# One product with B's row for two groups, in a selective-scan kernel on Trainium2

## The chip, the cores and the metric

The kernel runs on one core of a Trainium2 chip. The metric is the device time of one execution in microseconds; of the kernel before there are three runs, whose median is given below. A profile of a further execution shows each instruction of the engines: PE (TensorE, matmuls), DVE (VectorE), ACT (ScalarE), POOL (GpSimd) and SP, which here issues DMAs.

## What is computed

Four layers act on an image of 4 x 56 x 56 tokens with 96 channels. The first two hold a selective scan in four directions over the image; the last two are attention (linear, without a softmax) and a small quantised feed-forward net, per token. Nearly all of the time goes to the two layers with scans. Cut to what matters, each scan is, per image, direction, channel d (192 of them) and state s (16):

```python
d_a = jnp.exp(dt[..., None] * a)              # decay, per token, channel and state
d_b = dt[..., None] * b_ssm[:, :, None, :]    # B's row, the same for all channels

def step(h, inp):
    da_t, db_t, x_t, c_t = inp
    h = da_t * h + db_t * x_t[..., None]
    y_t = jnp.einsum('bds,bs->bd', h, c_t)
    return (h, y_t)
_, ys = jax.lax.scan(step, h0, xs)
```

The scan runs over 3136 tokens. The input of state s at a token is dt * x (one value for each channel) times B (one value for each state).

## The kernel before

**Tiling.** The 3136 tokens are cut into seven chunks of 448. A round takes one chunk, one half of the channels (e, 96 of 192) and a quarter of the states (q, four of 16): 96 x 4 = 384 pairs of channel and state, as three groups g of 128 partitions. With 2 layers x 4 images x 4 directions x 7 chunks x 2 halves x 4 quarters there are 1792 rounds. The order of the instructions on PE, ACT, DVE and POOL is written out by hand in `scans`; the other work of the layers (norms, projections, convolutions, attention) runs beside as "lanes", which step between the pieces of a round by a planner's budget.

**A round n**, engine by engine:

- PE spreads B's row over the 128 partitions: a matmul with a selection matrix leaves it in the PSUM tile `b` (L606, `spread_b`, one buffer). It is issued in `begin(n + 1)`, in the middle of the round before.
- POOL makes the input of group 2 in `begin` (L699): `du` (dt * x, from a DMA) times B's row from SBUF.
- DVE makes the inputs of groups 0 and 1 in `products` (L704): two instructions, each 128 x 448, `du` from SBUF times `b` from PSUM, written into the tile `h`. In `h` each group has its own row of 450 columns (`ROW`, 448 tokens and two more), so that the carry of the chunk before can lie beside the tokens. `tokens(h)` is the view of its 448 tokens by group.
- DVE then runs three scans in place (L711), one for each group: they read the decay `da[g]` (PSUM, one buffer per group) and the input in `h`, and overwrite `h` with the states. The state begins from the carry column beside the tokens.
- ACT computes the decay of the next round's group g after the scan of group g has freed `da[g]` (L663, `decay`), saves the last column of h (L681, `kept`) and puts the carry into the tile of round n + 2 (L676, `carried`). `h` has three buffers.
- POOL multiplies the states by C's row (L753, `hc`), and PE sums them over the states into `y` (L784, `add_up`), two rounds later. PE also runs matmuls on zeros (L771) in a number that the planner sets.

On DVE the order in a round is: product of group 0, product of group 1, scan 0, then what the lanes have for DVE, scan 1, scan 2. The products and the first scan always follow one another directly.

Of the kernel before, what the change touches and what calls it, by code (L numbers as in the profile page):

```python
# [16 lines left out]
ALU = mybir.AluOpType  # L17
# [15 lines left out]
CS = 448  # L33
# [134 lines left out]
class Net:  # L168
# [444 lines left out]
    def scans(self):  # L613
# [7 lines left out]
        nc, sp = self.nc, self.sp  # L621
        chunks = []
        for l in range(2):
            for i in range(NB):
                for n, (orient, rev) in enumerate(ORDER[l]):
                    for step in range(NCS):
                        ch = Step()
# [55 lines left out]
        def own(n):  # L683
            ch, e, q = rounds[n]
            return NQ * e + q in (OWN_TAIL if ch.l and ch.i else OWN)

        hs, bs = {}, {}

        def tokens(t):

            return self.groups(t, 2)[:, :, :CS]
# [8 lines left out]

        def products(n):
            ch, e, q = rounds[n]
            for g in range(3 if own(n) else 2):
                nc.vector.tensor_tensor(tokens(hs[n])[:, g], ch.du[e][:, g], bs[n], ALU.mult)  # L704

        def scan(n, g):
            ch, e, q = rounds[n]
# [13 lines left out]
        for n, (ch, e, q) in enumerate(rounds):  # L721
            r = NQ * e + q
            products(n)
            for c, o in steps(n):
                self.prepare(c, o)
# [669 lines left out]
```

## Time and profile before

| | us |
|---|---|
| median of 3 runs (8209.97 to 8214.31) | 8210.29 |
| the profiled execution, its own time | 8208.04 |
| its span, first to last instruction | 8206.3 |
| granted TensorE clock, mean over the span | 0.895 |
| L753 on POOL, 1792 products with C's row | 4883.6 |
| L663 on ACT, 5376 decays | 3353.4 |
| L784 on PE, 14336 sums over the states | 1924.6 |

The profile's first part gives, for each engine, the time in which it was busy, its share of the span, and the number of its instructions. A row of the groups reads: line, engine, operation, what is written and read, shape, count, then busy time in all and mean nanoseconds of one instruction, then the idle time of the engine just before such instructions and what ended it. An instruction's own length can overlap that of the next on the same engine, so the mean times the count can be more than the busy time. In the timeline each row gives the start and the length in microseconds from the span's start; rows of the same kind that follow one another are merged, with their count, and an idle gap before them is shown with what ended it. The rounds run from about 120 to 7926 us of the span; before lies the setup, after it the last lanes.

### The profile page before, as it was taken

Reading aid. Unit: us, or ns where it says so; the run is one execution under the profiler, and the core shown is the slowest. Engines: PE = TensorE matmul, PEld = TensorE weight load, DVE = VectorE, ACT = ScalarE, POOL = GpSimd, SP = SyncE. Lnnn points to the kernel's source line nnn. Section 1 sums busy time; section 2 is a strip of 40 time slices with the busy share of each in tenths; the row PEclk is TensorE's granted clock in tenths of the full one; section 3 lists DMA queues with packets and bytes.
Section 4 is the critical chain, followed back from the end, with each engine's and each line's share of the span. In section 5 each row is a group of like instructions: output and inputs, shape, how many; then the busy total and the mean of one; then the engine's idle time right before and its main releaser. Section 6 shows DMA issues by size and latency. Waiting matters only on the chain.

```text
span 8206.3 us, 113425 instructions
## 1 busy us (share of the span) xinstructions
PE 7235.6 (88%) x33734; PEld 2586.3 (32%) x33734; DVE 7506.3 (91%) x9558; ACT 6104.9 (74%) x12807; POOL 7170.8 (87%) x3991
## 2 busy tenths in 40 slices
PE   7889988889888988889898989998898988989897
PEld 3333333222332223322332224332343323433345
DVE  5999999999999999999999998999989999899961
ACT  5778877787778767886777866787767786677755
POOL 4999999999999998999999997999989998899950
PEclk8899989899999988999899998989889898898976
DMA  4566655567556665566565665555655555555531
GB/s 148 176 195 192 199 186 181 176 195 230 178 183 190 204 195 182 180 198 197 194 192 181 210 204 172 168 169 176 196 164 169 165 176 185 167 172 164 179 115 49
DMA packets 568241, 1467.55 MB, mean 179 GB/s; under 512 B 108034, under 2 KB 337156, under 8 KB 566756
## 3 DMA queue, kind: packets, MB, share of 16 engines
q1 hardware_dynamic: 566848, 1458.49, 56.2%
q8 instruction: 265, 4.34, 0.2%
q14 instruction: 356, 2.92, 0.1%
q10 hardware_dynamic: 772, 1.80, 0.1%
HBM read 1186.49 MB, written 273.47 MB: 178 GB/s over the span
## 4 chain that ended last, share of the span: by engine, by line
PE 34%; DVE 30%; ACT 16%; issue 13%; POOL 4%; DMA 2%; SPq 0%; DVEq 0%; POOLq 0%; ACTq 0%
DVE h L711 22%; PE y L784 7%; DVE h L704 7%; PE y L771 5%; ACT da L663 5%; PE y L780 4%; PE b L606 3%; POOL hc L753 2%; PE pp L486 2%; ACT L815 2%; PE pp L440 2%; PE ps L923 1%; PE ps L836 1%; PE ps L851 1%; ACT Y L791 1%
## 5 line engine op out<-in xcount | busy, mean ns | idle before, releaser
L711 DVE TENSOR_TENSOR_SCAN h<-da,h 128x449 f32<-128x449 f32 (+1 forms) x5376 | 5506.4, 1071 | 97.8 <-ACT da L663 83.5
L753 POOL TENSOR_TENSOR hc<-h,cb 128x1344 f32<-128x1344 f32 x1792 | 4883.6, 2725 | 616.2 <-DVE h L711 474.3
L663 ACT ACTIVATE da<-dt,na 128x448 f32<-128x448 f32 x5376 | 3353.4, 632 | 1116.2 <-DVE h L711 1086.0
L704 DVE TENSOR_TENSOR h<-du,b 128x448 f32<-128x448 f32 x3584 | 2016.1, 603 | 135.9 <-PE b L606 72.9
L784 PE MATMUL y<-hc,four 128*32 128x448 f32 x14336 | 1924.6, 612 | 17.5 <-POOL hc L753 17.5
L699 POOL TENSOR_TENSOR h<-du,cb 128x448 f32<-128x448 f32 x1792 | 1753.2, 978 | 70.4 <-ACT h L676 27.6
L771 PE MATMUL y<-w,zeros 128*96 128x448 bf16 x5112 | 1426.5, 398 | 0.0
L606 PE MATMUL b<-cf,sel 128*128 128x448 bf16 x1792 | 677.6, 378 | 691.4 <-DVE h L704 685.2
L771 PEld LDWEIGHTS <-zeros 128*96 128x96 bf16 x5112 | 633.6, 135 | 1178.0 <-issue 1018.7
L440 PE MATMUL pp<-U,wd 96*128 96x448 f32 x896 | 669.2, 835 | 11.7 <-issue 4.6
L784 PEld LDWEIGHTS y<-hc,four 128*32 128x32 f32 x14336 | 295.0, 113 | 1201.0 <-issue 684.6
L780 PE MATMUL y<-Y,ident 96*96 96x448 f32 x672 | 541.4, 895 | 36.3 <-ACT Y L791 19.2
L486 PE MATMUL pp<-cf,wd 12*96 12x448 f32 (+1 forms) x896 | 477.7, 615 | 87.7 <-ACT dtc L496 53.7
L681 ACT COPY carry<-h 128x3 f32<-128x3 f32 x1536 | 302.0, 197 | 261.5 <-DVE h L711 255.7
L511 POOL TENSOR_TENSOR duc<-dtc,U 96x896 f32<-96x896 f32 x224 | 482.9, 2156 | 4.4 <-ACT dtc L498 4.4
L791 ACT COPY Y<-y 96x448 f32<-96x448 f32 x448 | 342.1, 764 | 27.6 <-PE y L784 26.4
L676 ACT COPY h<-carry 128x3 f32<-128x3 f32 x1536 | 279.9, 182 | 51.5 <-POOL hc L753 48.4
L496 ACT ACTIVATE dtc<-pp,wd 96x448 f32<-96x448 f32 x448 | 281.5, 628 | 21.5 <-PE pp L486 17.4
L836 PEld LDWEIGHTS ps<-avg,w 96*112 96x112 f32 (+1 forms) x2008 | 264.6, 197 | 98.1 <-issue 55.4
L606 PEld LDWEIGHTS <-sel 128*128 128x128 bf16 x1792 | 184.7, 103 | 351.4 <-issue 282.4
L577 ACT COPY cf<-pp 64x448 f32<-64x448 f32 x448 | 235.6, 526 | 70.1 <-PE pp L599 61.5
L851 PEld LDWEIGHTS ps<-ident,rs 112*96 112x96 f32 x1808 | 224.0, 186 | 134.8 <-issue 92.2
(376 smaller groups left out, 5712.9 us busy)
## 6 DMA issues: line engine op xcount, KB each, us to landing
cb<-cd SPq DMA_DIRECT2D x896, 448.0 KB, 4.6
dt<-dd SPq DMA_DIRECT2D x448, 672.0 KB, 5.7
du<-dd SPq DMA_DIRECT2D x448, 672.0 KB, 5.7
dd<-dtc SPq DMA_DIRECT2D x672, 112.0 KB, 2.0
dd<-duc SPq DMA_DIRECT2D x672, 112.0 KB, 2.0
win<-m SPq DMA_DIRECT2D x252, 112.0 KB, 4.0
U<-u SPq DMA_DIRECT2D x112, 168.0 KB, 4.7
w<-z SPq DMA_DIRECT2D x84, 224.0 KB, 4.4
```

The source lines that it names most:

```text
L440: self.nc.tensor.matmul(ch.ps.rearrange("p (a b) -> p a b", b=HS), ch.par.wx[:, e], self.in_order(self.U[e], ch.orient, ch.c * CS, CS), st ...
L486: self.nc.tensor.matmul(ch.pd, ch.par.wt[rows, C * e : C * e + C], ch.cf[rows], start=True, stop=True)
L511: self.nc.gpsimd.tensor_tensor(in_rows(ch.duc), in_rows(ch.dtc), u[:, :, lo : lo + CS // HS], ALU.mult)
L606: self.nc.tensor.matmul(ps, self.sel[:, q], self.upper(ch.cf), start=True, stop=True)
L663: nc.scalar.activation(da[g][:, INNER], ch.dt[e][:, g], AF.Exp, scale=ch.par.na[:, e, q, g : g + 1])
L699: nc.gpsimd.tensor_tensor(tokens(hs[n])[:, 2], ch.du[e][:, 2], ch.cb[q][:, 1], ALU.mult)
L704: nc.vector.tensor_tensor(tokens(hs[n])[:, g], ch.du[e][:, g], bs[n], ALU.mult)
L711: nc.vector.tensor_tensor_scan(h[:, way], da[g][:, way], h[:, way], 0.0, ALU.mult, ALU.add)
L753: nc.gpsimd.tensor_tensor(hc, tokens(hs[n]), ch.cb[q][:, 0].unsqueeze(1).to_broadcast([128, NG, CS]), ALU.mult,)
L771: self.nc.tensor.matmul(self.y[:C], self.zeros[:, :C], self.some, start=False, stop=False)
L780: nc.tensor.matmul(o, w, self.in_order(a, ch.orient, ch.c * CS, CS), start=True, stop=False)
L784: nc.tensor.matmul(self.y[32 * n : 32 * n + 32], self.four, hc[:, g], start=n == 3, stop=n == 3 or q == NQ - 1,)
```

## The change

The two instructions of `products` become one. It writes both groups of h (two rows of 448, 450 apart), reads both groups of `du`, and reads B's row in PSUM twice: the view has a middle dimension of length m with a step of zero. (`own` is false in every round of this kernel, so m is 2.)

```diff
         def products(n):
             ch, e, q = rounds[n]
-            for g in range(3 if own(n) else 2):
-                nc.vector.tensor_tensor(tokens(hs[n])[:, g], ch.du[e][:, g], bs[n], ALU.mult)
+            m = 3 if own(n) else 2
+            b = bs[n].unsqueeze(1).to_broadcast([128, m, CS])
+            nc.vector.tensor_tensor(tokens(hs[n])[:, :m], ch.du[e][:, :m], b, ALU.mult)
```

Nothing else is changed. The built program has 1792 fewer instructions on DVE. The first scan still waits for DVE's own semaphore and for ACT's; the second, which waited for both, now waits for ACT's alone; the third waits for ACT's and POOL's, as before. The merged product carries the waits that the two had: PE's (B's row), ACT's (the carry) and, where a chunk begins, a DMA's (`du`).

## Prediction

> **What bounds the kernel now.** I read the page first: the sums by engine, then its costliest groups.
>
> ```profile
> span 8206.3 us, 113425 instructions
> PE 7235.6 (88%) x33734; PEld 2586.3 (32%) x33734; DVE 7506.3 (91%) x9558; ACT 6104.9 (74%) x12807; POOL 7170.8 (87%) x3991
> ...
> L711 DVE TENSOR_TENSOR_SCAN h<-da,h 128x449 f32<-128x449 f32 (+1 forms) x5376 | 5506.4, 1071 | 97.8 <-ACT da L663 83.5
> ...
> L704 DVE TENSOR_TENSOR h<-du,b 128x448 f32<-128x448 f32 x3584 | 2016.1, 603 | 135.9 <-PE b L606 72.9
> ```
>
> DVE is the fullest engine, and L704 and L711 are nearly all of it: two products and three scans in each of 1792 rounds. The stretches view puts the rounds between 120 and 7926 us of the span, with DVE busy for 7444.6 of those 7806 us: 4.356 us a round, and only 361 us idle in all. The three-engine balance (PE 88%, POOL 87%) doesn't change this: where DVE hardly idles, time added to it lengthens the run, up to those 361 us.
>
> Next I read the timeline of DVE alone, in the middle (start, length, both in us):
>
> ```profile
> 4020.40 1.12 DVE L704 TENSOR_TENSOR h<-du,b 128x448 f32<-128x448 f32 x2
> 4021.44 3.05 DVE L711 TENSOR_TENSOR_SCAN h<-da,h 128x449 f32<-128x449 f32 x3
> 4024.41 1.12 DVE L704 TENSOR_TENSOR h<-du,b 128x448 f32<-128x448 f32 x2
> ```
>
> A round without a stall takes 4.01 us (4020.40 to 4024.41), less than 2 x 0.603 + 3 x 1.071 = 4.42. So an instruction begins before the one ahead has ended: the pair ends at 4021.52, its first scan begins at 4021.44, 0.08 us sooner. Taken one by one, the second product starts 513 ns after the first and the scan 531 ns after that: 1044 ns from the first product to the scan. This is the number that the change replaces. 1150 of the 1792 rounds are within 0.1 us of this pace.
>
> **The part that goes.** One instruction and its fixed cost. What one longer instruction takes comes from these three lengths, all with one operand in PSUM:
>
> ```profile
> L227 DVE TENSOR_TENSOR in<-in,ps 96x384 f32<-96x384 f32 x2 | 1.1, 550 | 1.3 <-PE ps L226 1.3
> ...
> L405 DVE TENSOR_TENSOR qkv<-w,ps 96x288 f32<-96x288 f32 x2 | 0.9, 452 | 1.7 <-PE ps L404 1.7
> ```
>
> Slope (550 - 452) / 96 = 1.02 ns an element, so 448 more cost 457 ns. A first product without a stall takes 593 ns and the mean is 603, so the merged one takes 1050 to 1060; I take 1055. No product with two rows of 448 and a zero step over PSUM is in the trace. The bounds are 1050 and, if a new row paid the whole start again, 593 + 593 = 1186 ns. I take the low end's side because the one small product of this shape (L326, 96x8 as two rows of four, the second operand repeated by a zero step) takes 0.16 us, as does a product of one element: rows and the zero step cost nothing there.
>
> **The part that is added: a wait.** The first scan reads and overwrites group 0 of h. Before, group 0 was written by the first product, which ends half a microsecond ahead of the scan's start; the second product covered the wait. Merged, group 0 is not complete until the whole instruction is, and the built program has the scan wait for DVE's semaphore directly behind it. No DVE instruction of another kind stands between products and scan in any round, and the changed program has none there either, so nothing covers it. What a waiting instruction costs is shown in the setup:
>
> ```profile
> 3.60 0.16 DVE L342 TENSOR_TENSOR bn1t<-c 96x1 f32<-96x1 f32 x1 [0.85 <-DMA c<-in_c_dram]
> 3.68 0.15 DVE L342 TENSOR_TENSOR bn2t<-c 96x1 f32<-96x1 f32 x1
> ...
> 5.79 0.15 DVE L341 TENSOR_TENSOR bn1s<-bn1s,c 96x1 f32<-96x1 f32 x1
> 5.98 0.15 DVE L343 TENSOR_TENSOR bn1t<-bn1t,bn1s 96x1 f32<-96x1 f32 x1
> 6.17 0.15 DVE L344 TENSOR_TENSOR bn1t<-bn1t,c 96x1 f32<-96x1 f32 x1
> ```
>
> The two L342 are independent: the second starts 0.08 before the first ends. L341, L343 and L344 feed each other: each starts 35 ns after the end ahead (0.04 as rounded). But they wait for one semaphore. The scan waits for two (the product, and ACT's decay factors), and the sequencer takes the first as a step of its own (an event of 21 ns, 5286 of them on L711). In the trace this event, for the first product, comes 38 ns after that product's end. What follows a late event is seen where a product waits for B's row from PE:
>
> ```profile
> 983.91 0.36 PE L606 MATMUL b<-cf,sel 128*128 128x448 bf16 x1
> ...
> 984.31 0.62 DVE L704 TENSOR_TENSOR h<-du,b 128x448 f32<-128x448 f32 x1 [0.39 <-PE b L606]
> ```
>
> ```profile
> 295.11 0.57 PE L606 MATMUL b<-cf,sel 128*128 128x448 bf16 x1
> ...
> 295.79 0.62 DVE L704 TENSOR_TENSOR h<-du,b 128x448 f32<-128x448 f32 x1 [1.19 <-PE b L606]
> ```
>
> At 984 PE ends at 984.27 and the product starts 0.04 later, by a direct wait. At 295 an event lies between (PE ends at 295.68): 0.11 later. In all 19 waits of that kind the product starts 44 or 45 ns after the event. So the scan starts 38 + 21 + 44 = 103 ns behind the product's end; the bounds are 35 (the wait for the product is the direct one) and 108 (the event case as seen from PE). I take 103, since the program lists the two waits in the same order as before, where the product's was the event. Below nothing is a case of its own, under the rivals.
>
> A scan that starts on an idle engine also pushes the next a little: 1009 ns to the second scan in the 157 rounds where the first had stalled, against 1002: 7 ns.
>
> **Other moves.** The second scan loses its wait for DVE, which was long met: nothing. B's row on PE is freed when the products end; measured from the products' start that is 1.12 us before and 1.055 after, and the next row is due some 3 us later: nothing. The merged product takes over the second one's wait for ACT's carry, set 3 us ahead (copied at 4021.18, used at 4024.41): nothing, or 70 ns in some of the 87 waits for PE, 6 us at most. PE, ACT and POOL have the same instructions in the same order. On SP some DMA issues move a few places; DVE's waits for du come to 26.8 us, 19.2 of them at the first, so I put this at nothing, within 10 us either way.
>
> **The sum.** A round in step: 1055 + 103 + 7 - 1044 = 121 ns more. If all 1792 paid: 217 us. A round that stalls anyway, for ACT, PE or a DMA, takes the delay out of its stall. 386 rounds have an idle gap over 20 ns. If each covers itself, 1406 pay (170 us); if each covers the round ahead too, 1020 pay (123 us). I take 1200: 145 us. Against the profiled execution's own 8208.0 us (span 8206.3) that is 8353, and the median of the runs shown lies 2 us above that execution: 8355.
>
> **A rule against this sum.** The Trainium skill, VectorE: DVE Perf Modes, sections "The DRAIN you can't avoid" and "Rules for kernel authors", says that a semaphore after each chained Vector instruction costs nothing extra and that one should lower the count of instructions, not of semaphores. By it the scan would follow the merged product as it follows the second one now, 80 ns before its end: 975 - 1044 = -69 ns a round, 124 us faster. The setup's rows speak otherwise: 0.08 us before the end without a wait and 0.04 after it with one.
>
> **Rivals.**
> - The direct wait: 35 ns in place of 103. 53 ns a round; 1200 x 53 = 64 us: 8274. For it: the compiler may choose the waits' order. Against it: the list is unchanged.
> - A second start for the second row: 1186 + 110 - 1044 = 252 ns; so large a delay outlasts more of the stalls, so 1300 rounds: 328 us: 8538. For it only that the trace lacks the shape.
> - The other side: the wait is met when the product's last elements go in, not out, so that the scan overlaps as today. It decides once the scan starts less than 1044 - 1055 = -11 ns behind the product's end. At -80 it saves 1044 - 975 = 69 ns; rounds that stall give it back, so 1200 gain: 83 us, 8127. Against it: every waiting pair in the setup starts after the end.
> - Hidden anyway: ACT or PE sets the end and DVE's 361 idle us take all 217: 8210. For it: the whole chain of waits gives PE 34% and DVE 30%. Against it: the idle time lies in 386 rounds, and a stretch where 1150 rounds run in step has none to give.
>
> **How the numbers follow.** The forecast with its bounds (1020 rounds at 116 ns to 1406 at 131, so 8328 to 8394) has 0.70, the direct wait 0.15, the second start 0.05, the gain 0.07, hidden 0.03. The range reaches to the direct wait at the low end and to all 1792 rounds at 131 ns at the high: 8265 to 8445. What a measurement here can tell is 0.2%, 16 us: faster 0.07, within 0.03, slower 0.90.
>
> **What would show it.** In the changed profile: 1792 products of 1050 to 1060 ns; scan 0 starting about 0.10 us after their end in the timeline, each such round 4.13 us long; DVE's busy sum as before within some 40 us (a round in step is busy for 4.03 us of its 4.13), its idle time higher by over 100 us; less waiting of DVE for ACT and PE. A start of the scan before the product's end, or a product above 1.1 us, would prove the step on the wait or on the rows wrong; rounds of 4.13 us in a run of 8210 would prove the count of paying rounds wrong.

## The result, and the profile after

The changed kernel takes 8341.32 us (median of 5 runs, 8337.12 to 8343.85) against 8210.29: 1.0156 of the kernel before, with a 95% interval of 1.0142 to 1.0171. It is slower, by 131 us; 145 were forecast. The profiled execution has a span of 8342.1 us, 135.8 more than before.

The page's sums and its two rows of DVE, which answer to those shown of before (L705 is the product, L712 the scan; every line behind the product has moved by one):

```profile
span 8342.1 us, 110355 instructions
...
PE 7294.0 (87%) x33734; PEld 2599.9 (31%) x33734; DVE 7527.7 (90%) x7766; ACT 6117.9 (73%) x12807; POOL 7176.5 (86%) x3991
...
L712 DVE TENSOR_TENSOR_SCAN h<-da,h 128x449 f32<-128x449 f32 (+1 forms) x5376 | 5523.0, 1076 | 255.3 <-ACT da L663 73.1
...
L705 DVE TENSOR_TENSOR h<-du,b 128x896 f32<-128x896 f32 x1792 | 1906.3, 1064 | 128.4 <-PE b L606 52.1
```

DVE has 1792 instructions fewer, and its busy time is the same within 22 us (7527.7 against 7506.3). What grew is the idle time in front of the scans: 255.3 us, of which only 73.1 are ACT's; before they were 97.8 and 83.5. Most of the rest, 166 us, is gaps of 0.10 to 0.11 us in front of the first scan of 1615 rounds, which the row puts down to no engine; the timeline shows what they are.

This is DVE in the middle of the changed kernel, round by round:

```profile
4019.24 1.06 DVE L705 TENSOR_TENSOR h<-du,b 128x896 f32<-128x896 f32 x1
4020.40 3.05 DVE L712 TENSOR_TENSOR_SCAN h<-da,h 128x448 f32<-128x448 f32 x3
4023.37 1.06 DVE L705 TENSOR_TENSOR h<-du,b 128x896 f32<-128x896 f32 x1
4024.54 3.05 DVE L712 TENSOR_TENSOR_SCAN h<-da,h 128x448 f32<-128x448 f32 x3
```

The product ends at 4020.30 and the first scan begins at 4020.40. At the other end of the round nothing has changed: the scans end at 4023.45 and the next product begins at 4023.37, 0.08 us sooner. Over all rounds the median gap behind the product is 103 ns (the middle half 103 to 104), where it was an overlap of 79 to 80 ns; the product lasts 1064 ns; a round in step takes 4.142 us in place of 4.013.

Round by round against the kernel before, the account closes. The 1150 rounds that were in step before took 177.6 us more together, the other 641 took 33.3 us less (their stalls gave the delay back), and before the first round and after the last one 4.2 us each were saved: 177.6 - 33.3 - 8.5 = 135.8 us, the difference of the spans. Of the 1150 rounds about 1100 are in step in both kernels and took 140 us of the 177.6, 127 ns each; nearly 50 others now stall and took 38 us. The 8.5 us around the rounds are not put down to the change: in the 13 profiles of this case the first product starts anywhere between 112.8 and 120.3 us, and the stretch behind the last one lasts 273.6 to 286.9 us.

The granted TensorE clock is a little lower, 0.887 on the mean against 0.895. It doesn't explain the loss: DVE's products waited less for PE than before (52.1 us against 72.9).

### The profile page after: what moved, and what is told of

It is laid out like the page before. It is cut to its first block, busy times and chain, and to the rows that moved or that the text cites. A ratio compares the mean times of both kernels' runs of the same rounds, so it can differ in the third digit from the quotient of the medians.

```text
span 8342.1 us, 110355 instructions
## 1 busy us (share of the span) xinstructions
PE 7294.0 (87%) x33734; PEld 2599.9 (31%) x33734; DVE 7527.7 (90%) x7766; ACT 6117.9 (73%) x12807; POOL 7176.5 (86%) x3991
## 3 DMA queue, kind: packets, MB, share of 16 engines
q14 instruction: 333, 2.73, 0.1%
## 4 chain that ended last, share of the span: by engine, by line
PE 43%; DVE 31%; ACT 12%; issue 10%; DMA 2%; POOL 2%; SPq 0%; DVEq 0%; POOLq 0%; ACTq 0%
DVE h L712 21%; DVE h L705 9%; PE y L785 9%; PE y L772 7%; PE y L781 5%; PE b L606 4%; ACT da L663 3%; PE pp L486 2%; PE pp L440 2%; PE ps L852 2%; PE ps L837 2%; PE ps L924 1%; ACT L816 1%; PE ps L810 1%; POOL hc L754 1%
## 5 line engine op out<-in xcount | busy, mean ns | idle before, releaser
L712 DVE TENSOR_TENSOR_SCAN h<-da,h 128x449 f32<-128x449 f32 (+1 forms) x5376 | 5523.0, 1076 | 255.3 <-ACT da L663 73.1
L705 DVE TENSOR_TENSOR h<-du,b 128x896 f32<-128x896 f32 x1792 | 1906.3, 1064 | 128.4 <-PE b L606 52.1
L486 PE MATMUL pp<-cf,wd 12*96 12x448 f32 (+1 forms) x896 | 498.3, 639 | 98.0 <-ACT dtc L496 57.1
L511 POOL TENSOR_TENSOR duc<-dtc,U 96x896 f32<-96x896 f32 x224 | 482.8, 2155 | 9.3 <-ACT dtc L498 9.3
```

The lines of the kernel that those rows point to most:

```text
L486: self.nc.tensor.matmul(ch.pd, ch.par.wt[rows, C * e : C * e + C], ch.cf[rows], start=True, stop=True)
L511: self.nc.gpsimd.tensor_tensor(in_rows(ch.duc), in_rows(ch.dtc), u[:, :, lo : lo + CS // HS], ALU.mult)
L705: nc.vector.tensor_tensor(tokens(hs[n])[:, :m], ch.du[e][:, :m], b, ALU.mult)
L712: nc.vector.tensor_tensor_scan(h[:, way], da[g][:, way], h[:, way], 0.0, ALU.mult, ALU.add)
```

## The experiments

The theory: the time is lost in the wait of the first scan for the product directly ahead of it, which two separate products had covered. The rival: the merged instruction itself is what costs (its length, its two rows, the zero step). A second question came up on the way: is there an order in which the wait is covered again, and what is the merge worth then? Ratios are against runs of the kernel before on the same chip, with the 95% interval; "in step" is the median round without a stall, from the trace.

| run | median, us | ratio to before | in step, us |
|---|---|---|---|
| the changed kernel | 8341.32 | 1.0156 (1.0142 to 1.0171) | 4.142 |
| 1: two products, reversed | 8456.15 | 1.0302 (1.0285 to 1.0318) | 4.204 |
| 2: merged, scan of group 2 first | 8283.02 | 1.0086 (1.0072 to 1.0100) | 3.947 |
| 3: merged, product one scan early | 8586.10 | 1.0460 (1.0445 to 1.0474) | 3.947 |
| 4: two products, scan of group 2 first | 8381.42 | 1.0206 (1.0192 to 1.0220) | 4.012 |
| 5: as 2, old order in one round of eight | 8275.17 | 1.0067 (1.0048 to 1.0086) | 3.948 |
| 6: as 2, POOL's group 2 ahead of L511 | 8262.33 | 1.0051 (1.0034 to 1.0069) | 3.947 |
| 7: as 6, two products | 8306.66 | 1.0109 (1.0090 to 1.0127) | 4.012 |
| 8: merged, the scan with one wait | 8612.19 | 1.0480 (1.0464 to 1.0497) | 4.071 |
| 9: as 6, L511 in two halves | 8177.24 | 0.9950 (0.9932 to 0.9967) | 3.947 |
| 10: as 9, two products | 8230.96 | 1.0027 (1.0017 to 1.0037) | 4.012 |
| 11: as 10, old order of the scans | 8205.24 | 0.9995 (0.9986 to 1.0004) | 4.012 |

**1. The wait without the merge.** Two products, but group 1 first, so that the scan of group 0 follows the product that feeds it:

```diff
-            for g in range(3 if own(n) else 2):
+            for g in (1, 0):
                 nc.vector.tensor_tensor(tokens(hs[n])[:, g], ch.du[e][:, g], bs[n], ALU.mult)
```

> Two products as in the kernel before, but group 1 first and group 0 second, so that the first scan's input comes from the instruction directly ahead of it. No merged instruction and no zero step. Theory of the exposed wait: the scan starts 103 ns after the second product's end in place of 80 ns before it, 183 ns a round and 7 ns at the second scan; with some 1200 rounds that pay, about 228 us: 8438 us (8400 to 8480). Rival, that the time comes from the merged instruction itself (its length, its rows, its zero step): nothing of that is here, so 8210 us within 20.

Measured: 8456.15 us, inside the range of the forecast. DVE's timeline in this run:

```profile
4020.92 1.13 DVE L704 TENSOR_TENSOR h<-du,b 128x448 f32<-128x448 f32 x2
4022.15 3.06 DVE L711 TENSOR_TENSOR_SCAN h<-da,h 128x449 f32<-128x449 f32 x3
4025.13 1.12 DVE L704 TENSOR_TENSOR h<-du,b 128x448 f32<-128x448 f32 x2
4026.36 1.09 DVE L711 TENSOR_TENSOR_SCAN h<-da,h 128x449 f32<-128x449 f32 x1
```

The pair ends at 4022.05 and the scan begins at 4022.15: the gap of the changed kernel, with no merged instruction in the program. The same work in another order costs 246 us. This is the theory's case alone, and the rival, which had 8210, falls.

**2 to 4. The wait covered.** In run 2 the scans go in the order 2, 0, 1 (group 2's input comes from POOL and not from the merged product), with ACT's decays in the same order:

```diff
+        turn = (2, 0, 1)
...
-            for g in range(NG):
-                if g == 1:
+            for j, g in enumerate(turn):
+                if j == 1:
                     yield "C", n, r
...
                 scan(n, g)
-                if g == 2:
+                if j == 2:
                     kept(n)
```

> The merged product, and the scans in the order 2, 0, 1 (the decays on ACT in the same order). Group 2 comes from POOL, so its scan covers the wait for the merged product. Theory of the exposed wait: the merged product takes 984 ns of a round (1064 less 80) in place of 1044 before, the round in step is 3.95 us, 60 ns under the kernel before in some 1200 rounds: 8138 us; POOL's product is needed one scan sooner and can be late in the 224 rounds with its larger product, so 8110 to 8210. Rival, that the merged instruction is what costs: 8341 us within 30, whatever the order.

In run 3 the order stays, and the next round's merged product moves between scans 1 and 2:

```diff
-            products(n)
+            if n == 0:
+                products(n)
...
+                if g == 2 and n + 1 < len(rounds):
+                    products(n + 1)
                 scan(n, g)
```

> The merged product of the next round between scans 1 and 2 of this one: scan 2 covers its wait, and POOL's product is needed no sooner. Theory of the exposed wait: as with the scan of group 2 first, 60 ns a round under the kernel before: 8138 us (8110 to 8175). B's row on PE is needed one scan sooner, which would show as DVE's waiting for L606. Rival, that the merged instruction is what costs: 8341 us within 30.

Run 4 is run 2 with the two products of before, as a control for the order:

> Two products as before, and the scans in the order 2, 0, 1: a control for the order alone. Theory of the exposed wait: before, no wait was exposed, so the order has nothing to cover: 8210 us, within 25. Rival, that the order of the scans helps by itself (so that a gain with the merged product would be no proof): clearly under 8190 us.

In step all three do what the theory said: 3.947 us with the merged product covered, 65 ns under the 4.012 of two products (60 were expected). All three totals miss their forecasts by far, because in each the order calls up another wait. The scans' waits for POOL before, and the waits of DVE in run 2, longest first (total in us, times, longest):

```profile
DVE h L711 <- POOL h L699: 12.4, 14, 2.0
```

```profile
DVE h L712 <- POOL h L699: 191.6, 194, 2.4
DVE h L712 <- ACT da L663: 92.9, 137, 2.3
```

Before, the scans waited 12.4 us for POOL; now it is 191.6, because POOL's group 2 is wanted two scans sooner (the expectation has one). 152.6 us of it lie in one round of eight, r = 4 (r counts the eight rounds of a chunk, 4e + q), behind POOL's larger product (L511, `times_u`, which makes dt * x for a later chunk, both halves of the channels at once, once in eight rounds). Run 4 has the same stall, 176.3 us with two products, and so the pair is the fair comparison: 8381 with two products, 8283 with one. The control's own expectation, 8210 us, was wrong: the order alone costs 171 us. It does not help, which is what it was there to tell. In run 3 the waits are others:

```profile
DVE h L712 <- ACT da L663: 265.0, 228, 2.2
DVE h L705 <- PE b L606: 175.9, 108, 5.1
```

B's row is wanted sooner, as its expectation named, and late in 108 rounds. The waits for ACT were not expected. In program order ACT now has one product less of time between a round's last scan and the next round's first one to fit in the lanes' work; that this is their cause is argued, not shown.

**5. Another order in the one round that stalls:** `enumerate((0, 1, 2) if r == 4 else turn)`.

> The merged product with the scans in the order 2, 0, 1, but 0, 1, 2 in the one round of eight whose group 2 POOL makes late (r = 4, behind its larger product L511; 153 of the 192 us that the first scan waited for POOL lie there). Theory of the exposed wait: that round costs what it does with the merged product and the old order (4.38 us on average) in place of 4.93, 224 times: 123 us under the 8283 us of the order 2, 0, 1 throughout, so 8160 us (8130 to 8200). Rival, that the order shifts other work and the stall only moves: 8250 us or more.

Measured: 8275.17 us, 8 less than run 2, where 123 less were forecast. The rival holds: the scans' waits for POOL fell from 191.6 us to 77.7, but their waits for ACT rose from 92.9 to 161.7 us (64 of them in r = 4, where the decay of group 0 is now wanted one scan sooner behind the round before), and 54 of those for POOL lie in r = 5.

**6 and 7. POOL's order.** `times_u` (L511) is called behind `begin(n + 1)` in place of ahead of it, once with the merged product and once with two:

```diff
         elif o == -5:
-            self.times_u(ch)
             ch.dtd = self.park(ch.dtc)
...
             begin(n + 1)
+            for c, o in steps(n):
+                if o == -5:
+                    self.times_u(c)
```

> The merged product with the scans in the order 2, 0, 1, and POOL makes the next round's group 2 ahead of its larger product (L511) in place of behind it. Theory: the stall on POOL goes (round r = 4 falls from 4.93 us to about 4.28, 224 times, 146 us) and the exposed wait stays covered: 8137 us (8100 to 8180), faster than the kernel before. Rival, that covering the wait does not pay outside the rounds in step: 8210 us or more.

> As the run before (order 2, 0, 1, POOL's group 2 ahead of its larger product), but with two products. The difference of the two is the merge alone with its wait covered. Theory: 1044 ns from product to scan in place of 984 and 18 ns less at a scan with one wait fewer, so 60 to 70 ns in some 1200 to 1500 rounds: this one 75 to 105 us slower than the run before, 8210 to 8260 us. Rival, that the order and POOL do all of it and the merge nothing: the two within 20 us of one another.

Measured: 8262.33 and 8306.66 us, both above their forecasts. Round r = 4 fell to 4.293 us as forecast, but r = 5 rose from 4.126 to 4.558 with 89 us of waiting for POOL: the stall moved by one round, since POOL was still 2.2 us behind. The pair differs by 44 us, less than the 75 to 105 forecast, and the merge is again the faster of the two.

**8. The two parts of the wait.** ACT copies the carry of round n + 1 right behind that round's first decay. The product waits for that copy, and the scan behind it then has one wait only, for DVE:

```diff
                 hs[n] = sp.tile([128, WIDE], F32, name="h", bufs=3)
+
+        def carry_in(n):
+
+            if n < len(rounds):
+                ch, e, q = rounds[n]
                 if not ch.step:
                     return
...
                 decay(n + 1, g)
+                if g == 0:
+                    carry_in(n + 1)
```

> The merged product and the scans in the old order, but ACT copies the carry of the next round right behind the first decay of that round, so that the product's own wait for ACT covers the first scan's, and that scan waits for DVE alone. Theory of the two steps of the wait: the gap behind the product falls from 103 ns to 35 in the six rounds of seven that have a carry, the round in step from 4.142 to 4.074 us; the product now waits for ACT 1.1 us sooner than the scan did, which gives a part back: 8290 us (8260 to 8335). Rival, that the 103 ns are the product's own drain whatever waits: a gap of 103 ns and 8341 us or more.

Half of it held. The product and the first scan of two kinds of round (L710 is the product, L717 the scan):

```profile
4991.90 1.06 DVE L710 TENSOR_TENSOR h<-du,b 128x896 f32<-128x896 f32 x1
4993.06 3.05 DVE L717 TENSOR_TENSOR_SCAN h<-da,h 128x448 f32<-128x448 f32 x3
...
5018.22 1.06 DVE L710 TENSOR_TENSOR h<-du,b 128x896 f32<-128x896 f32 x1
5019.31 3.06 DVE L717 TENSOR_TENSOR_SCAN h<-da,h 128x449 f32<-128x449 f32 x3
5022.29 1.06 DVE L710 TENSOR_TENSOR h<-du,b 128x896 f32<-128x896 f32 x1
```

The scan at 4993 belongs to a first chunk, which has no carry (448 columns and not 449), and keeps both waits; the one at 5019 has one. In all 1536 rounds with a carry the gap behind the product is 33 to 36 ns, and no event lies between; in the 256 without, the event is there and the gap is 102 to 104 ns in 235 of them, longer in the rest. So the 68 ns between 103 and 35 belong to the second wait, which the sequencer takes as a step of its own. The round in step is 4.071 us. The total, 8612.19 us, was missed by over 300. The product's row on the page and ACT's longest wait for POOL say why:

```profile
L710 DVE TENSOR_TENSOR h<-du,b 128x896 f32<-128x896 f32 x1792 | 1916.3, 1069 | 521.0 <-ACT h L681 460.9
```

```profile
ACT h L681 <- POOL h L704: 525.0, 515, 6.3
```

The carry goes into the same tile as POOL's product of group 2 and now stands behind it, so ACT waited for POOL (525.0 us) and the product for ACT (460.9 us). Before, POOL's product of group 2 was needed by the last scan only.

**9 to 11. A version that beats both.** In run 9 POOL's larger product is cut into its two halves (e = 0 and 1), two rounds apart, on top of run 6, and the transfers that store it are split likewise; only in an image's last chunk do they stay together, since the next image's input overwrites theirs:

```diff
+    def halves(self, ch, o):
+        return (0, 1) if ch.last and o == -5 else (0,) if o == -5 else (1,) if o == -3 and not ch.last else ()
...
             begin(n + 1)
             for c, o in steps(n):
-                if o == -5:
-                    self.times_u(c)
+                for e_ in self.halves(c, o):
+                    self.times_u(c, e_)
```

> The merged product, scans in the order 2, 0, 1, POOL's group 2 ahead of its larger product, and that product (L511) cut into two halves, two rounds apart, so that POOL is never 2.2 us behind (in an image's last chunk both halves stay together). Theory: the 89 us that the first scan waited for POOL in round r = 5 go for the most part, that round falls from 4.56 to about 4.25 us, 224 times: 70 us, so 8190 us (8160 to 8220), at or just under the kernel before. Rival, that POOL has no room left at 3.95 us a round (its work is 2.73 + 0.98 + 0.27 = 3.98 us): the stall only spreads over more rounds, 8245 us or more.

Runs 10 and 11 take the merge away, and then the order of the scans too:

> As the run before, with two products: the difference is the merge alone with its wait covered, where POOL stalls least. Theory: 60 to 66 ns in the 950 rounds or so that run in step, and less in the rest: 55 to 90 us slower than the run before. Rival, that POOL takes the gain back: within 25 us of it.

> Two products and the scans in the old order 0, 1, 2, with POOL's two changes alone (group 2 ahead of the larger product, that product in two halves): a control for the run that beat the kernel before. Theory: before, the scan waited for POOL 12 us in all, so there is little to gain: 8200 us (8185 to 8225). Rival, that POOL's changes and not the merge made the faster version: 8180 us or less.

Run 9 takes 8177.24 us, 0.9950 of the kernel before (0.9932 to 0.9967); it and run 11 lie inside their forecasts. DVE's timeline there:

```profile
4100.57 1.06 DVE L722 TENSOR_TENSOR h<-du,b 128x896 f32<-128x896 f32 x1
4101.55 3.05 DVE L729 TENSOR_TENSOR_SCAN h<-da,h 128x449 f32<-128x449 f32 x3
4104.52 1.06 DVE L722 TENSOR_TENSOR h<-du,b 128x896 f32<-128x896 f32 x1
```

The product ends at 4101.63, the scan (of group 2) begins at 4101.55: the overlap of before, with one instruction fewer, and 3.95 us from product to product. The scans' waits for POOL are down to 83.0 us, and round r = 5 to 4.218 (4.25 was expected). Its controls say which part does it: POOL's changes alone give 0.9995, no difference; with the order of the scans 1.0027, slower; with the merge on top 0.9950. The merge with its wait covered is worth 54 us here (8230.96 - 8177.24, just under the 55 to 90 forecast; 98 between runs 4 and 2, 44 between 7 and 6), the merge with its wait exposed costs 131.

## Why the prediction was right

**The bound.** DVE was read as the engine to which time can't be added unseen. It held: the rounds that were in step before took 177.6 us more, and those that stalled gave back only 33.3.

**The merged instruction.** Forecast 1055 ns from the slope of the rows, measured 1064: the second row and its zero step pay no second start, and the rival with 1186 ns is out. The 9 ns are a small error of size; the slope was taken from shapes of 288 and 384.

**The added wait.** Forecast 103 ns; measured 103, and in the same three parts: in the changed kernel the event comes 38 or 39 ns after the product's end, lasts 21, and the scan starts 43 or 44 ns behind it. The bound of 35 was the right figure for a wait that is taken directly, as run 8 showed, and the rival that rested on it fails only because the scan has two waits. The rival on the other side, with the scan starting before the product's end, is out in every round: not one gap is under 100 ns in the changed kernel. The 7 ns at the second scan were measured as forecast (1009 against 1002).

**The count of rounds that pay.** In step a round costs 129 ns more where 121 were forecast; the difference is the product's 9 ns, within 1 ns. From the first round's product to the last one's the rounds took 144.3 us more, which is 144.3 / 0.129 = 1119 full payments; 1200 were taken, out of bounds of 1020 and 1406, and about 1100 rounds are in fact in step in both kernels. That the rounds' sum is met so closely (144 against 145) is luck in part: a larger price and a smaller count nearly cancel. The 8.5 us around the rounds, which no step had and which lie within the spread of the profiles, are most of what is left to the measured 131 to 136.

**The rule that spoke against it.** The Trainium skill (VectorE: DVE Perf Modes, sections "The DRAIN you can't avoid" and "Rules for kernel authors") says that a semaphore after each chained Vector instruction costs nothing extra. The prediction's estimate by it was 124 us faster. The measurement decides, and here the wait is not free: 183 ns lie between a scan that starts 80 ns before the end ahead and one that starts 103 ns after it, and run 1 paid for that with no other change. The part of the rule on lowering the count of instructions holds once the wait is covered: 65 ns a round in runs 2, 6 and 9.

**What the profile was to show.** Products of 1050 to 1060 ns (1064, just above), a gap of about 0.10 us (0.103), rounds of 4.13 us (4.142), DVE busy as before within 40 us (21 more) with over 100 us more idle (484 in place of 361 us between the first and the last scan), less waiting for ACT and PE (the scans for ACT 73.1 us in place of 83.5, the products for PE 52.1 in place of 72.9): all seen but for the 4 ns of the product.

## What to carry to other kernels

Two small instructions ahead of a consumer of the first are a pipeline: the second hides the wait for the first. Before merging them, look at what follows directly and what it reads; if it reads the merged result, put an instruction between that does not. Here the saved start is worth 65 ns a round (4.012 against 3.947 us), and the exposed wait takes back 195 (4.142 against 3.947), three times as much. And an order that covers one wait calls for its other inputs sooner, so look at how much room the engine that makes them has over several rounds, not at its lead in one.

## What had not been expected

- How little room POOL has. These are its three products of the rounds in the changed kernel:

```profile
L754 POOL TENSOR_TENSOR hc<-h,cb 128x1344 f32<-128x1344 f32 x1792 | 4885.3, 2726 | 752.8 <-DVE h L712 595.7 <-ACT Y L792 29.8 <-PE y L772 19.5
L699 POOL TENSOR_TENSOR h<-du,cb 128x448 f32<-128x448 f32 x1792 | 1754.2, 979 | 65.9 <-ACT h L676 23.0 <-DMA du<-dd 19.1 <-DMA cb<-cd 5.4
L511 POOL TENSOR_TENSOR duc<-dtc,U 96x896 f32<-96x896 f32 x224 | 482.8, 2155 | 9.3 <-ACT dtc L498 9.3
```

  It needs 2.73 + 0.98 us a round and 2.16 us (L511) once in eight, 3.98 us a round on average, against 3.947 us of a round in step. Its 87% of the span hides this: moving its deadline forward by two scans turned 12.4 us of waiting into 191.6, and removing the stall in one round moved it to the next (run 6) until the larger product was cut (run 9).
- The cost of a second wait on an instruction: 68 ns when the first of the two is met last, shown by taking it away (run 8). Where that wait has long been met, no cost of it is seen here. Run 7's expectation counted on 18 ns at a scan with one wait fewer, but the first scan lasts 1082 ns in both run 6 and run 7. What goes with lengths of 17 to 19 ns more is the instruction ahead: in the kernel before, a scan that overlaps another scan ahead of it lasts 1062 ns, and one that overlaps an instruction of any other kind 1078 to 1081, the second scan behind a lane's instruction as much as the first behind the product; a product lasts 593 ns behind a scan and 610 behind a product. What causes this was not tried.
